# VectorE's last dt step and convolution taps a third of a round later, and VectorE side work in every third of a round

## The chip, the cores and the metric

The kernel runs on one core of a Trainium2 chip (trn2). The metric is device time in microseconds (us): the median of several executions of the same program. A core has five engines that each run their own list of instructions in order: TensorE (PE in the profile), VectorE (DVE), ScalarE (ACT), GpSimd (POOL) and SyncE (SP), which here only issues DMAs. They meet through semaphores.

## The reference

Two layers follow each other on x of shape (8, 384, 32, 32), all in fp32. The first is a group norm, a Mamba block and an MLP, added to x; the second a group norm and a mixture of four experts, of which the two best are used, added again. The change lies in the Mamba block, whose core is:

```python
xz = t @ in_proj_w.T
xm, z = jnp.split(xz, 2, axis=-1)
xc = sum((xp[:, k:k + L, :] * conv_w[:, k] for k in range(K))) + conv_b   # K = 3, causal; xp is xm padded
xc = jax.nn.silu(xc)
dt, Bm, Cm = jnp.split(xc @ x_proj_w.T, [dt_rank, dt_rank + d_state], axis=-1)
dt = jax.nn.softplus(dt @ dt_proj_w.T + dt_proj_b)
dA = jnp.exp(jnp.einsum('bld,dn->bldn', dt, A))
dBu = jnp.einsum('bld,bln->bldn', dt * xc, Bm)
# per token: hst = dA_t * hst + dBu_t ;  y_t = sum over the 16 states of hst * C_t
y = (ys + xc * D) * jax.nn.silu(z)
t = gelu((y @ out_proj_w.T) @ mlp_w1.T + mlp_b1) @ mlp_w2.T + mlp_b2
```

## The kernel before

**Tiling.** The 8 x 1024 tokens are cut into 16 chunks of 512 (`i`; even chunks are the first half of an image, odd ones the second, which start from a carried state). The 768 inner channels are 6 blocks of 128 (`d`), the 16 states 4 groups of 4 (`s`). One round (`r`) is one (chunk, block, state group): 24 rounds (`k`) make a chunk, and the loop has 384 rounds. After it a tail finishes the MLP and the experts' first layer, and `experts` computes the experts' second layer from DRAM.

**One round** scans 4 x 128 rows of 512 tokens. GpSimd multiplies `du = dxr * b` for the next round (`drive`, L742). ScalarE makes four decays exp(dt * A) (`decay`, L734): two into the PSUM tile `da_A`, two one after the other into the single PSUM tile `da_B`, so that the second has to wait for the scan that reads the first. VectorE does four scans (`scan`, L750; the four are numbered j = 0 to 3, of which 2 and 3 use `da_B`) and multiplies half of the result by c (`read_out`, L754); GpSimd does the other half. TensorE sums the states into `y` (`sum_states`, L776) at the head of the next round.

**Side work.** All else (in_proj, convolution, dt, gates, norms, out_proj, MLP, the experts' first layer) is written as generators. Each step `yield`s an engine, a cost and a wait: the wait is the least number of *thirds* of a round after the step before. A round calls `side` three times, at fixed places among the scans:

```python
scan(r, 2); drive(r + 1); decay(r, 3); batch()
side("PE", "DVE", *act, act=ACT_FIRST)          # first third
scan(r, 0); scan(r, 3)
side("PE", *act)                                # middle third
decay(r + 1, 2); scan(r, 1); read_out(V, ...); read_out(G, ...); decay(r + 1, 0); decay(r + 1, 1)
side("PE", "DVE", "ACT", act=ACT_LAST)          # last third
```

`side` gives the named engines credit (2.7 us of TensorE, 0.6 us of VectorE for each third) and issues the steps that are due, the most urgent first. A round in which `batch` has put a Silu or Gelu batch on ScalarE (two table loads and three activations) issues no other ScalarE step in its first two thirds. The order on each engine is therefore fixed when the program is built. A step that opens a PSUM bank ("bank") also needs one of the four banks of `ps_g` to be free at its place in the order; the step that calls `free()` gives it back.

**The two steps that the change touches.** `delta` (L391 and on) makes dt: a matmul into a bank (L396), ScalarE's Relu, Exp and Ln (L400 to L402), then VectorE's `scalar_tensor_tensor` (L404), which gives the bank back. Behind that, GpSimd multiplies dt by xc (`dtx`, L407), and both are written to DRAM and read back repeated. `conv` makes the convolution: three matmuls into a bank (L295), ScalarE's first tap (L307, L308, for even chunks' convolutions also the edge, L311 and L312), then VectorE's two taps (L314, L315), after which the bank is free. Other VectorE side steps are the norm (L267, L283), the additions to x1 (L522 to L528), and the first group norm's statistics (L243).

Of the kernel before, what the change touches and what calls it, by code (L numbers as in the profile page):

```python
# [112 lines left out]
def layer0(ctx, tc, io, ident, cmean, eps, dram, x1_dram, gn1, logits, r_dram, group_norm):  # L113
# [8 lines left out]
    V, S, G, PE = nc.vector, nc.scalar, nc.gpsimd, nc.tensor  # L122
# [68 lines left out]
    def exp_ln_tables():  # L191
        S.preload_act_table_set(EXP_LN_SET)
# [4 lines left out]
    def bank(name):  # L197
        held[0] += 1
        return ps_g.tile([P, T], F32, name=name, tag="g")

    def free():
        held[0] -= 1
# [87 lines left out]
    def in_proj(i, block):  # L290
        assert i in normal
        w = w_in.take("in_proj", block)
        g = bank("g_in")
        for j in range(J):
            PE.matmul(g, lhsT=w[:, j, :], rhs=xt[i][:, j, :], start=(j == 0), stop=(j == J - 1))  # L295
        return g

    def conv(i, d, at_once=False):
        half = i % NH
        while i not in normal or i > 1 and i - 2 not in out_done or not w_in.turn("in_proj", d):  # L300
            yield "-", 0, 1
        yield "bank", 3, 0
        g = in_proj(i, d)
        yield "ACT", 1.1 if half else 1.5, 1
        w = lambda k: conv_w[:, d, k:k + 1]
        acc = pxc.tile([P, T], F32, name="xc")
        S.copy(acc[:, 0:2], (edge if half else edge0)[:, d, :])  # L307
        S.activation(acc[:, 2:T], g[:, 0:T - 2], AF.Identity, bias=conv_b[:, d:d + 1], scale=w(0))  # L308
        if half + 1 < NH:
            e = edge[:, d, :]  # L310
            S.activation(e, g[:, T - 2:T], AF.Identity, bias=conv_b[:, d:d + 1], scale=w(0))  # L311
            S.activation(e[:, 0:1], g[:, T - 1:T], AF.Identity, bias=e[:, 0:1], scale=w(1))  # L312
        yield "DVE", 1.5, 1
        V.scalar_tensor_tensor(acc[:, 1:T], g[:, 0:T - 1], w(1), acc[:, 1:T], ALU.mult, ALU.add)  # L314
        V.scalar_tensor_tensor(acc, g, w(2), acc, ALU.mult, ALU.add)  # L315
        free()
        if at_once:
            yield "ACT", 0.6, 1
            S.activation(acc, acc, AF.Silu)
            xc[i, d] = acc  # L320
        else:
            accs[i, d] = acc
# [51 lines left out]
    def load_b(i, s):  # L374
        bt[i, s] = load_rows("b", i, s)
# [4 lines left out]
    def written(name, i, d, what):  # L380
        there = dram.tile([P, T], F32, name=f"{name}_dram{i}_{d}")
        nc.sync.dma_start(there, what)
        return there

    def repeat(into, there, j):

        rows = there[j * (P // Q):(j + 1) * (P // Q), :]
        nc.sync.dma_start(into, rows.unsqueeze(1).to_broadcast([P // Q, Q, T]))

    def delta(i, d):  # L390
        while i not in dbc or making_dt:  # L391
            yield "-", 0, 1
        making_dt.append((i, d))
        yield "bank", 1, 1
        g = bank("g_dt")
        PE.matmul(g, lhsT=w_dt[:, d * P:(d + 1) * P], rhs=dbc[i][0:DTR, :], start=True, stop=True)  # L396
        projected.add((i, d))
        yield "ACT", 2.0, 1
        dt = p1.tile([P, T], F32, name="dt")
        S.activation(dt, g, AF.Relu, bias=b16[:, d:d + 1], scale=-1.0)  # L400
        S.activation(dt, dt, AF.Exp, bias=top, scale=-1.0)
        S.activation(dt, dt, AF.Ln, bias=1.0)  # L402
        yield "DVE", 0.75, 1
        V.scalar_tensor_tensor(dt, g, b_dt[:, d:d + 1], dt, ALU.add, ALU.max)  # L404
        free()
        dtx = p1.tile([P, T], F32, name="dtx")
        G.tensor_tensor(dtx, dt, xc[i, d], ALU.mult)  # L407
        yield "-", 0, 1
        there = written("dtr", i, d, dt)
        yield "-", 0, 1  # L410
        there_x = written("dxr", i, d, dtx)
        making_dt.clear()
        last = i * per + d * NG - 1
        yield "-", 0, 1
        while issued["B"] < last - NG:
            yield "-", 0, 1
        dtr[i, d] = {}
        pair = dtr[i, d]["B"] = p2.tile([P, 2, T], F32, name="dtr_b")
        for k in range(2):
            repeat(pair[:, k, :], there, 2 + k)  # L420
        yield "-", 0, 1
        while issued["drive"] < last - NG:
            yield "-", 0, 1
        dxr[i, d] = p2.tile([P, Q, T], F32, name="dxr")
        for j in range(Q):
            repeat(dxr[i, d][:, j, :], there_x, j)
        yield "-", 0, 1
        while issued["A"] < last:
            yield "-", 0, 1
        yield "-", 0, 1  # L430
        pair = dtr[i, d]["A"] = p1.tile([P, 2, T], F32, name="dtr_a")
        for k in range(2):
            repeat(pair[:, k, :], there, k)
# [367 lines left out]
    def begin(*new, rank=2):  # L801
        tasks.extend(Task(t, rank) for t in new)
# [66 lines left out]
    with tc.manual_schedule():  # L869
        w_in = Stream(pw_in, [("in_proj", k) for k in in_order()])  # L870
        begin(statistics(0))
        drain()
        begin(norm(0))
        drain()
        S.preload_act_table_set(SILU_SET)
        begin(*(conv(0, d, at_once=True) for d in range(ND)), x_proj(0))
        drain(lambda: len(xc) == ND)
        exp_ln_tables()
        drain()
        load_b(0, 0)  # L880
        load_c(0, 0)
        begin(delta(0, 0))
        drain()
        for s in range(1, NG):
            load_b(0, s)
            load_c(0, s)
        begin(delta(0, 1), rank=0)
        begin(*(gate(0, d) for d in range(3)))
        begin(silus(zs, gates, [(0, d) for d in range(3)]))
        begin(norm(1))  # L890
        w_out = Stream(pw_out, [("out_proj", k) for i in range(NCH) for k in range(2 * J)])
        w_1 = Stream(pw_1, [("mlp_w1", u) for i in range(NCH) for u in range(NF)])
        w_2 = Stream(pw_2, [("mlp_w2", 4 * j + 2 * half + k) for i in range(NCH) for half in range(2)
                            for j in range(J) for k in range(2)])
        seed(0, 0)
        w_e = Stream(pw_e, [("e_w1", u) for i in range(NCH) for u in range(E * J)])
        drive(0)
        for j in (2, 0, 1):
            decay(0, j)
        begin(out_lane(), rank=1.5)  # L900
        begin(hidden_lane(), rank=3)
        begin(second_lane(), rank=2.5)
        begin(expert_lane(), rank=4)

        batched = [False]

        def side(*engines, act=None):
            slot[0] += 1
            credit["PE"] = min(credit["PE"] + PE_SLOT, 4)
            credit["DVE"] = min(credit["DVE"] + DVE_SLOT, 2)  # L910
            if act is not None:
                credit["ACT"] = act + min(credit["ACT"], 0)
            issue({e: ENOUGH[e] for e in engines})

        def batch():

            ready = [t for t in tasks if t.engine == "batch" and t.ready <= slot[0]]
            batched[0] = bool(ready) and not batched[0]
            if batched[0]:
                min(ready, key=Task.urgency).resume()  # L920

        for r in range(rounds):
            i, d, s = at(r)
            k = r % per
            more = r + 1 < rounds
            plan(i, k)
            if r > 0:
                sum_states(r - 1)
            scan(r, 2)
            if more:  # L930
                drive(r + 1)
            decay(r, 3)
            batch()
            act = () if batched[0] else ("ACT",)
            side("PE", "DVE", *act, act=ACT_FIRST)
            scan(r, 0)
            scan(r, 3)
            last_token(G.tensor_copy, r, BB, du[r][:, BB, :])
            side("PE", *act)
            if more:  # L940
                decay(r + 1, 2)
            scan(r, 1)
            read_out(V, r, A, da[r, "A"])
            last_token(V.tensor_copy, r, A, da[r, "A"])
            read_out(G, r, BB, du[r][:, BB, :])
            if more:
                decay(r + 1, 0)
                decay(r + 1, 1)
            if s == 0 and r > 0:
                finish(*at(r - 1)[:2])  # L950
                seed(i, d)
            side("PE", "DVE", "ACT", act=ACT_LAST)
        sum_states(rounds - 1)
        finish(NCH - 1, ND - 1)
        begin(last_x1(), route(), rank=0)
        drain()
# [116 lines left out]
```

## Time and profile before

| what | us |
|---|---|
| three executions: median (lowest to highest) | 4099.31 (4096.35 to 4102.39) |
| profiled execution | 4110.87 |
| its span, first to last instruction | 4109.0 |
| first scan of the loop / first scan of the last round, from the span's start | 76.0 / 3400.0 |
| loop in between, for each of 383 rounds | 8.68 |
| tail (MLP and experts' first layer) | 3400 to 3607 |
| experts' second layer | 3607 to 4109 |

Busy times of the whole span: PE 3709.2, DVE 3032.3, POOL 2782.5, ACT 2422.7 us. A profile's row gives an engine, an instruction, its count, busy time and mean duration, and after the bar the time that its engine sat idle just before it with what ended that idle time. Idle time of an engine costs nothing by itself: what counts is whether the work that waits lies on the path that sets the round's length.

### The profile page before, as it was taken

To read this page: it belongs to the slowest core of one execution; us is meant where nothing else is said; L and a number is where in the kernel's file an instruction comes from. 1 tells how busy PE (TensorE), PEld (TensorE's weight loads), DVE (VectorE), ACT (ScalarE), POOL (GpSimd) and SP (SyncE) were. 2 spreads that over 40 slices of the span, in tenths; PEclk is the share of its full clock that TensorE was granted. 3 is DMA by queue.
4 is the path that set the end of the run, shared out by engine and by line. 5 is a ranking of instruction groups with operands and counts; after the bars stand their busy time and mean duration, and the time that the engine had idled before them with its cause. 6 is when DMAs were issued, how large, how long until landed. Compare 5 with 4: busy or idle time off the path is not lost. (4 is left out here: it accounts for less than half of the span.)

```text
span 4109.0 us, 35186 instructions
## 1 busy us (share of the span) xinstructions
PE 3709.2 (90%) x10294; PEld 1385.4 (34%) x10294; DVE 3032.3 (74%) x3081; ACT 2422.7 (59%) x3762; POOL 2782.5 (68%) x1070
## 2 busy tenths in 40 slices
PE   6678888999999999998999989898999899889999
PEld 2123223333333333333333333333333334334444
DVE  4888888878887878888878787878787781165552
ACT  4657676767686768676766677677767663200000
POOL 3898988788877888888878888888878881000000
PEclk8779898999999999999999999999999999899999
DMA  4444444464545454555455444555554543465552
GB/s 127 134 137 134 152 142 158 143 201 164 172 150 180 164 167 151 192 166 175 154 187 172 159 163 159 181 167 166 165 167 155 163 161 96 169 222 189 185 188 98
DMA packets 372499, 665.31 MB, mean 162 GB/s; under 512 B 40252, under 2 KB 151228, under 8 KB 370132
## 3 DMA queue, kind: packets, MB, share of 16 engines
q1 hardware_dynamic: 342352, 610.02, 45.8%
q10 hardware_dynamic: 29956, 53.05, 3.4%
q8 instruction: 83, 1.36, 0.1%
q14 instruction: 108, 0.88, 0.1%
HBM read 535.90 MB, written 127.01 MB: 161 GB/s over the span
## 5 line engine op out<-in xcount | busy, mean ns | idle before, releaser
L742 POOL TENSOR_TENSOR du<-dxr,b 128x2048 f32<-128x2048 f32 x384 | 1740.9, 4534 | 25.1 <-PE y L776 15.1
L754 POOL TENSOR_TENSOR du<-du,c 128x1024 f32<-128x1024 f32 x384 | 905.8, 2359 | 229.2 <-DVE du L750 199.7
L734 ACT ACTIVATE da_A<-dtr_a,w_a_log 128x512 f32<-128x512 f32 x768 | 527.6, 687 | 280.3 <-DVE du L754 122.1
L734 ACT ACTIVATE da_B<-dtr_b,w_a_log 128x512 f32<-128x512 f32 x768 | 527.3, 687 | 260.4 <-DVE du L750 207.2
L478 PE MATMUL hid<-tt,mlp_w 128*128 128x512 f32 x1152 | 541.5, 613 | 63.8 <-ACT h L482 46.7
L776 PE MATMUL y<-du,sel 128*32 128x512 f32 x3072 | 466.3, 642 | 134.1 <-DVE du L754 92.2
L750 DVE TENSOR_TENSOR_SCAN du<-da_B,carry,du 128x512 f32<-128x512 f32 x384 | 488.4, 1272 | 123.2 <-ACT da_B L734 114.8
L619 PE MATMUL e_hid<-xn,e_w 128*128 128x512 f32 x1080 | 519.2, 627 | 55.4 <-ACT r L623 37.9
L295 PE MATMUL g_in<-xt,in_proj 128*128 128x512 f32 x1152 | 554.7, 619 | 13.8 <-ACT xt L287 7.0
L517 PE MATMUL acc<-h,mlp_w 128*128 128x512 f32 x1152 | 543.4, 614 | 24.5 <-ACT h L493 15.9
L750 DVE TENSOR_TENSOR_SCAN du<-da_B,du 128x512 f32<-128x512 f32 x384 | 464.7, 1210 | 130.5 <-ACT da_B L734 114.0
L1026 PE MATMUL acc<-r,w_e_w 128*128 128x512 f32 x1152 | 496.6, 594 | 13.1 <-DVE r L1023 13.1
L750 DVE TENSOR_TENSOR_SCAN da_A<-da_A,carry,du 128x512 f32<-128x512 f32 x384 | 489.3, 1274 | 9.6 <-ACT da_A L734 9.0
L750 DVE TENSOR_TENSOR_SCAN da_A<-da_A,du 128x512 f32<-128x512 f32 x384 | 465.5, 1212 | 27.0 <-ACT da_A L734 25.0
L754 DVE TENSOR_TENSOR du<-da_A,c 128x1024 f32<-128x1024 f32 x384 | 470.3, 1225 | 13.2
L478 PEld LDWEIGHTS hid<-tt,mlp_w 128*128 128x128 f32 x1152 | 215.8, 193 | 366.5 <-issue 239.1
L517 PEld LDWEIGHTS acc<-h,mlp_w 128*128 128x128 f32 x1152 | 216.6, 195 | 343.9 <-issue 247.7
L295 PEld LDWEIGHTS g_in<-xt,in_proj 128*128 128x128 f32 x1152 | 210.0, 194 | 353.5 <-issue 255.1
L619 PEld LDWEIGHTS e_hid<-xn,e_w 128*128 128x128 f32 x1080 | 207.4, 199 | 356.2 <-issue 250.3
L1026 PEld LDWEIGHTS acc<-r,w_e_w 128*128 128x128 f32 x1152 | 219.6, 191 | 290.1 <-issue 287.3
L456 PE MATMUL g_out<-xc,out_proj 128*128 128x512 f32 x576 | 284.0, 641 | 32.9 <-DVE xc L783 32.9
L407 POOL TENSOR_TENSOR dtx<-dt,xc 128x512 f32<-128x512 f32 x96 | 122.1, 1272 | 217.5 <-DVE dt L404 217.5
(129 smaller groups left out, 3030.2 us busy)
## 6 DMA issues: line engine op xcount, KB each, us to landing
dxr<-dxr_dram SPq DMA_DIRECT2D x384, 256.0 KB, 4.7
mlp_w<-in_mlp_w SPq DMA_DIRECT2D x384, 192.0 KB, 2.9
dtr_b<-dtr_dram SPq DMA_DIRECT2D x192, 256.0 KB, 4.2
dtr_a<-dtr_dram SPq DMA_DIRECT2D x192, 256.0 KB, 3.2
r_dram<-r ACTq DMA_DIRECT2D x192, 256.0 KB, 3.5
r<-r_dram SPq DMA_DIRECT2D x64, 768.0 KB, 4.8
in_proj<-in_in_proj SPq DMA_DIRECT2D x192, 192.0 KB, 4.0
e_w<-in_e_w SPq DMA_DIRECT2D x192, 192.0 KB, 3.2
```

What stands on the lines that cost most here:

```text
L295: PE.matmul(g, lhsT=w[:, j, :], rhs=xt[i][:, j, :], start=(j == 0), stop=(j == J - 1))
L407: G.tensor_tensor(dtx, dt, xc[i, d], ALU.mult)
L456: PE.matmul(g, lhsT=w[:, d, :], rhs=xc[i, 3 * k + d], start=(k + d == 0), stop=(k == 1 and d == 2))
L478: PE.matmul(g, lhsT=w[:, j, :], rhs=tt[i][:, j, :], start=(j == 0), stop=(j == J - 1))
L517: PE.matmul(g, lhsT=w[:, n, :], rhs=hs[mine[n]], start=(k + n == 0), stop=(k == 1 and n == 2))
L619: PE.matmul(h, lhsT=w[:, j, :], rhs=xn[:, j, :], start=(j == 0), stop=(j == J - 1))
L734: S.activation(out, dtr[i, d][pair][:, j % 2, :], AF.Exp, scale=neg_a[:, d, j, s:s + 1])
L742: G.tensor_tensor(du[r], dxr[i, d], wide(bt[i, s].unsqueeze(1), [P, Q, T]), ALU.mult)
L750: V.tensor_tensor_scan(a if j < 2 else b, a, b, start, ALU.mult, ALU.add)
L754: engine.tensor_tensor(du[r][:, js, :], h, wide(ct[i, s].unsqueeze(1), [P, 2, T]), ALU.mult)
L776: PE.matmul(y[j * m:(j + 1) * m, :], lhsT=sel, rhs=h[:, j, :], start=False, stop=(s == NG - 1), tile_position=(0, j * m), skip_group_check ...
L1026: PE.matmul(acc[j], lhsT=e2[:, e, d, j, :], rhs=r[:, d, :], start=(e + d == 0), stop=(e + d == E + J - 2))
```

## The change

`conv`'s and `delta`'s VectorE steps wait two thirds of a round behind ScalarE's step where they waited one, and the middle third of a round may issue VectorE steps too.

```diff
@@ conv
             S.activation(e[:, 0:1], g[:, T - 1:T], AF.Identity, bias=e[:, 0:1], scale=w(1))
-        yield "DVE", 1.5, 1
+        yield "DVE", 1.5, 2
         V.scalar_tensor_tensor(acc[:, 1:T], g[:, 0:T - 1], w(1), acc[:, 1:T], ALU.mult, ALU.add)
         V.scalar_tensor_tensor(acc, g, w(2), acc, ALU.mult, ALU.add)
         free()
@@ delta
         S.activation(dt, dt, AF.Ln, bias=1.0)
-        yield "DVE", 0.75, 1
+        yield "DVE", 0.75, 2
         V.scalar_tensor_tensor(dt, g, b_dt[:, d:d + 1], dt, ALU.add, ALU.max)
         free()
@@ the loop over rounds
             last_token(G.tensor_copy, r, BB, du[r][:, BB, :])
-            side("PE", *act)
+            side("PE", "DVE", *act)
             if more:
                 decay(r + 1, 2)
```

## The prediction

> **What bounds the kernel now.** I read the busy times by stretch, then who waited for whom inside the loop, then single rounds. The stretches are first scan to last (76 to 3400 us), tail, and experts' second layer (us; then busy us and instruction count of PE, PEld, DVE, ACT, POOL; granted clock, DMA share, GB/s):
>
> ```profile
> 76.00:3400.00 3324.00, 2994.14 (x8645) 1073.60 (x8646) 2720.27 (x2698) 2332.43 (x3612) 2771.78 (x1053) 0.95 0.50 163
> 3400.00:3607.00 207.00, 172.54 (x410) 74.16 (x409) 27.46 (x54) 61.96 (x93) 2.76 (x3) 0.90 0.43 145
> 3607.00:4109.00 502.00, 496.38 (x1152) 219.33 (x1152) 266.45 (x303) 0.00 (x0) 0.00 (x0) 0.99 0.51 171
> ```
>
> In the loop TensorE is busy 90%, GpSimd 83%, VectorE 82%, ScalarE 70%: none is full, all are near it, and a round of 8.68 us on average is longer than the 7.08 us (4.53 + 2.36 + 0.19) that GpSimd's own row sums ask. What lies between is waiting. VectorE's and GpSimd's waits in the loop:
>
> ```profile
> DVE du L750 <- ACT da_B L734: 228.4, 234, 3.9
> DVE dt L404 <- ACT dt L402: 153.3, 80, 4.1
> DVE xc L314 <- ACT edge L312: 57.9, 29, 3.2
> DVE xc L314 <- ACT xc L308: 49.9, 36, 2.6
> ...
> POOL du L754 <- DVE du L750: 195.1, 106, 5.0
> POOL dtx L407 <- DVE dt L404: 160.0, 78, 4.5
> POOL carry L759 <- DVE du L750: 150.7, 89, 4.1
> ...
> PE y L776 <- DVE du L754: 92.2, 45, 6.5
> ```
>
> VectorE stands 153.3 + 57.9 + 49.9 = 261 us before the steps that the change moves, and GpSimd 160 us before dtx. These sums invite a forecast of -260 us. Two timelines say what a wait is worth. First round 9 of chunk 8, VectorE and ScalarE (start, duration, idle before in brackets):
>
> ```profile
> 1800.77 1.21 DVE L750 TENSOR_TENSOR_SCAN du<-da_B,du 128x512 f32<-128x512 f32 x1
> 1803.41 0.75 DVE L314 SCALAR_TENSOR_TENSOR xc<-g_in,w_conv_w,xc 128x511 f32<-128x511 f32 x1 [1.43 <-ACT xc L308]
> ...
> 1804.86 1.22 DVE L750 TENSOR_TENSOR_SCAN da_A<-da_A,du 128x512 f32<-128x512 f32 x1
> ...
> 1808.35 1.23 DVE L754 TENSOR_TENSOR du<-da_A,c 128x1024 f32<-128x1024 f32 x1
> ...
> 1802.60 0.78 ACT L308 ACTIVATE xc<-g_in,w_conv_b,w_conv_w 128x510 f32<-128x510 f32 x1
> 1803.27 0.69 ACT L734 ACTIVATE da_B<-dtr_b,w_a_log 128x512 f32<-128x512 f32 x1
> ```
>
> VectorE waits 1.43 us for the convolution's first tap, and ScalarE makes the decay of scan 3 only behind that tap. Then the end of round 17, a dt step:
>
> ```profile
> 1880.06 0.75 DVE L404 SCALAR_TENSOR_TENSOR dt<-g_dt,w_dt_b,dt 128x512 f32<-128x512 f32 x1 [3.00 <-ACT dt L402]
> 1881.99 1.22 DVE L750 TENSOR_TENSOR_SCAN du<-da_B,du 128x512 f32<-128x512 f32 x1 [1.19 <-ACT da_B L734]
> 1883.26 1.23 DVE L750 TENSOR_TENSOR_SCAN da_A<-da_A,du 128x512 f32<-128x512 f32 x1
> ```
>
> The scan behind dt waits as well, for a decay that stands behind Relu, Exp and Ln.
>
> **What the Trainium skill says.** "TensorE: Matmul & The Clock Gate", on the array and its queues (Architectural detail), has ScalarE's and VectorE's queues as strict FIFO. The trace agrees: 3.00 us at dt held a scan and everything else behind it. "Perfetto Trace Analysis", Optimizing Tensor Performance, Matmuls, wants matmul groups to rotate through PSUM banks so that evacuation of one overlaps the next; here four banks are shared, and the change holds two kinds of bank longer. "ScalarE: Activation LUTs", What ACT_TABLE_LOAD costs, gives 1283 ns for a table load; the trace's row has 1283 ns too.
>
> **The change part by part.** It adds and removes no instruction: the built orders hold the same ones, and the tail keeps all of its matmuls (36 hidden, 36 second, 48 expert, 18 out_proj). Only waits can change, within the 3324 us. The orders show:
>
> - dt, 95 times in the loop: 80 move from the last third to the first of the next round, thus behind scan 2; 15 from a first third to the middle one, behind scans 0 and 3. GpSimd's dtx moves behind the 4.53 us drive.
> - convolution taps, 90: 58 first and 32 last thirds become 20 first, 50 middle, 20 last.
> - the x1 additions, norm and statistics spread over the three thirds; the DMA writes of dt come one third later on SP, and for 7 chunks the next chunk's first dt about a round later, at round 19 where its data is read from round 23: two rounds or more of cover, for transfers of 4.7 us.
>
> *Convolution.* In round 9 above, in the new order: scan 0 follows scan 2 (to 1803.1), the decay for scan 3 is there at 1803.96, scan 3 ends at 1805.25, the taps (0.75 + 0.75) at 1806.75, scan 1 at 1807.9. The read-out starts there and not at 1808.35: -0.45 us. So of 1.43 us of wait a third is gained; the rest comes back as a wait for `da_B`. Walking rounds 6 to 12 this way by hand, with the rows' durations and both orders, from the end of round 5: the even chunk takes 64.4 us in the old order (64.5 in the trace) and 62.3 in the new, the odd one 1.0 less. 8 even and 7 odd chunks: -16 - 7 = -23 us. The walk takes TensorE and GpSimd as in time.
>
> *dt.* In round 17's case scan 2 still starts at 1881.99, dt follows at 1883.2, scan 0 at 1883.95 where it was at 1883.26: +0.7. Done for the 81 dt steps that stand before scan 2, leaving out the very first, single values run from -0.7 to +2.9 (gain positive) and the sum is a loss of 9 us: the wait for Ln becomes one for the decay right behind Ln. Half of these lie beside a ScalarE or TensorE path; I take +5, with 0 and +57 (81 x 0.7) as ends.
>
> *GpSimd.* Its 160 us at dtx go, but the read-out that follows needs scan 3, and 195 + 151 us of waits for it show who is late. Only in rounds 0 to 4 of odd chunks, at 7.0 us a round, is GpSimd the path: 0.7 us there, 7 times: -5. Ends 0 and -40 (a quarter of 160).
>
> *The norm.* In odd chunks the dt of round 22 and the norm's 1.81 us stand together behind one wait (round 22 takes 12.1 us). Apart, the norm fills that wait: about -1.4, 7 times: -10.
>
> *The later dt of even chunks.* Round 17 (11.8 us on average) loses it, but rounds 18 and 19 get it and four groups of expert matmuls in one round: I put the three, 30.5 us before in chunk 8, at 29.5 at least. Seven times -1: -7, ends -21 and +14.
>
> *Banks.* dt's and the convolution's banks come back a third (2.9 us) later. In the built orders all four banks are held at the end of 326 thirds where it was 207, and a TensorE group opens a bank freed in the same third, with no other free, 177 times where it was 86 (behind dt 40 for 7, behind taps 30 for 6). These 91 add a wait of TensorE on VectorE. No row shows its price: nothing if TensorE is behind anyway, as between rounds 12 and 21; one scan and dt, about 2 us, if it is in step. With half out of sight and 0.4 for the others: 91 x 0.2 = +18. Ends 0 and +91 (1.0 each). What hides them is TensorE's lag; where that is gone, y is late and the read-out's buffer with it.
>
> Sum: -23 + 5 - 5 - 10 - 7 + 18 = -22 us. The profiled execution takes 4110.9 (1.9 outside its span), which would become 4089; it stood 11.6 above the median of the runs, so the forecast for the median is 4077 us. Without the guessed terms it is -23 - 10, with them at their worst +129 (57 + 14 + 91 - 33).
>
> **The rivals.**
>
> *TensorE starves at the banks.* The place is the first and middle thirds, where a group now opens a bank that VectorE has just given back. TensorE has 330 us of idle time in the loop, 10%, so waits land on it soon; in favour also that single rounds get more uneven (in chunk 8 round 18 keeps 2 us of matmuls and 19 gets 12). Against: in sums over two rounds the loads of both orders agree within 0.2%. The other terms give -40, so it decides from 40/91 = 0.44 us for each added case; at 0.9 us the time is 4099 - 40 + 82 = 4141.
>
> *The waits go for good.* If scans had their decays ready whenever VectorE passes dt and taps, the 261 us would go; about 110 would return as waits for `da_B` (half of 228): 4099 - 150 = 3950. The two timelines speak against it.
>
> *Nothing measurable.* TensorE, whose groups fill rounds 12 to 21, sets the time, and the gains are waited out there: 4099. About 0.2% (8 us) is what a measurement of this kernel tells from no change.
>
> *The change doesn't do what it says:* excluded by the built orders.
>
> **How the numbers follow.** The forecast, 4077 with 4045 to 4091 around it, gets 0.44; waits gone for good (below 4040) 0.07; nothing 0.12; the banks, or dt on the path at its upper end, 0.37, from 4108 up. So faster 0.51, same 0.12, slower 0.37. For 8 in 10 the range is 4010 to 4150: a tenth is left below, and above it only the bank term at its full price with dt's.
>
> **What would show it.** Right: the waits at L404 and L314 nearly gone, dtx without wait, `da_B` waits of VectorE up by some 100 us, rounds 6 to 12 of even chunks 2 us shorter. Wrong in the sum: TensorE's matmul waits behind `dt L404`, 20 us now, and behind taps grown by over 40 us; or `da_B` waits grown by more than 261 us, the moved waits and more.

## The result, and the profile after

The changed kernel takes 4063.81 us (median of 6, 4055.27 to 4069.07) beside 4097.83 us for the kernel before on the same chip (6, 4093.61 to 4102.65): a ratio of 0.9913, with a 95% interval of 0.9899 to 0.9927, or 34 us less. The forecast was 4077.

The busy times by stretch for the kernel after, in the columns of the prediction's first fence:

```profile
76.00:3359.00 3283.00, 2975.97 (x8646) 1079.95 (x8647) 2715.10 (x2699) 2328.63 (x3613) 2775.44 (x1054) 0.95 0.50 165
3359.00:3565.00 206.00, 169.75 (x409) 72.63 (x408) 27.39 (x53) 61.65 (x93) 2.56 (x2) 0.93 0.43 147
3565.00:4067.00 502.00, 496.70 (x1152) 219.46 (x1150) 266.43 (x303) 0.00 (x0) 0.00 (x0) 0.99 0.50 171
```

All of the gain lies in the loop, 3324 us before and 3283 now; the tail (207 and 206 us) and the experts' second layer (502) stay. The instructions are the same and the busy times move little, most of all TensorE's, by 18 us of 2994. So it is mainly waits that went. Here are waits of VectorE, GpSimd and TensorE in the loop, after:

```profile
DVE du L750 <- ACT da_B L734: 416.6, 283, 5.8
...
POOL du L742 <- PE y L776: 55.8, 39, 4.2
POOL dtx L407 <- ACT da_B L734: 32.9, 29, 2.8
...
PE e_hid L619 <- DVE dt L404: 4.2, 5, 0.9
PE g_in L295 <- DVE dt L404: 3.9, 6, 0.7
```

The waits in front of dt (L404) and the taps (L314), 261 us before, are gone from the list, but the scans' wait for `da_B` rose by 188 us (228.4 to 416.6). GpSimd's 160 us in front of dtx became 54 us (33 of them put down to a decay), and its wait in front of the drive, for TensorE's `y`, grew from 15 to 56 us. Some 370 us of waits left their places, and the loop of this profile is 41 us shorter.

Round 9 of chunk 8, the prediction's example, now reads like this on VectorE and ScalarE:

```profile
1781.91 1.21 DVE L750 TENSOR_TENSOR_SCAN du<-da_B,du 128x512 f32<-128x512 f32 x1
...
1785.35 1.22 DVE L750 TENSOR_TENSOR_SCAN du<-da_B,du 128x512 f32<-128x512 f32 x1 [1.11 <-ACT da_B L734]
1786.49 0.72 DVE L314 SCALAR_TENSOR_TENSOR xc<-g_in,w_conv_w,xc 128x511 f32<-128x511 f32 x1
...
1789.17 1.23 DVE L754 TENSOR_TENSOR du<-da_A,c 128x1024 f32<-128x1024 f32 x1
...
1783.95 0.78 ACT L308 ACTIVATE xc<-g_in,w_conv_b,w_conv_w 128x510 f32<-128x510 f32 x1
1784.63 0.69 ACT L734 ACTIVATE da_B<-dtr_b,w_a_log 128x512 f32<-128x512 f32 x1
```

The taps find their data, and scan 3 waits 1.11 us for the decay that stands behind ScalarE's first tap. From the first scan to the read-out it is 7.26 us; it was 7.58 before.

Where the rounds changed is told by the start of each round's first scan. These are means over chunks 2 to 14, in us, of the four kernels that the explanation needs most, each from one profile. (The profiled execution of the kernel before took 4110.9 us, 13 above the median, so its column is somewhat long.)

| rounds | before, even / odd | after, even / odd | e2, even / odd | e12, even / odd |
|---|---|---|---|---|
| 0 to 4 | 41.4 / 36.0 | 37.9 / 40.1 | 40.3 / 36.0 | 39.9 / 36.0 |
| 5 | 11.0 / 10.1 | 10.4 / 10.8 | 10.2 / 10.1 | 10.3 / 10.1 |
| 6 to 12 | 62.0 / 65.5 | 59.9 / 64.9 | 59.0 / 63.4 | 59.0 / 63.5 |
| 13 to 16 | 32.0 / 33.1 | 32.7 / 34.2 | 31.8 / 33.5 | 31.8 / 33.5 |
| 17 to 20 | 38.0 / 37.4 | 35.1 / 38.3 | 37.8 / 37.0 | 35.0 / 37.0 |
| 21 to 23 | 26.5 / 28.6 | 26.4 / 26.4 | 26.0 / 28.6 | 26.2 / 29.0 |
| chunk | 210.9 / 210.6 | 202.3 / 214.7 | 205.1 / 208.6 | 202.1 / 209.1 |

Even chunks gained 8.6 us each and odd ones lost 4.1. The change touches both alike, so something that differs between them must carry much of the result. The built orders show what: in even chunks of the kernel after, norm's mean comes in round 23 where it was 22, the next chunk's first dt in round 19 where it was 17, and in odd chunks norm's last additions in round 5 where they were in round 1. Nothing in the diff asks for that; it follows from the planner.

### The profile page after: what moved, and what is told of

It is laid out like the page before. It is cut to its first block, busy times and chain, and to the rows that moved or that the text cites. A ratio compares the mean times of both kernels' runs of the same rounds, so it can differ in the third digit from the quotient of the medians.

```text
span 4067.3 us, 35077 instructions
## 1 busy us (share of the span) xinstructions
PE 3688.2 (91%) x10294; PEld 1390.4 (34%) x10294; DVE 3026.9 (74%) x3081; ACT 2418.6 (59%) x3762; POOL 2785.6 (68%) x1070
## 5 line engine op out<-in xcount | busy, mean ns | idle before, releaser
L295 PE MATMUL g_in<-xt,in_proj 128*128 128x512 f32 x1152 | 561.3, 626 | 28.9 <-ACT xt L287 23.4
L517 PE MATMUL acc<-h,mlp_w 128*128 128x512 f32 x1152 | 535.8, 612 | 26.2 <-ACT h L482 15.9
L478 PE MATMUL hid<-tt,mlp_w 128*128 128x512 f32 x1152 | 529.8, 601 | 21.6 <-ACT h L482 10.2
L1023 DVE TENSOR_TENSOR r<-r,spread 128x1536 f32<-128x1536 f32 x64 | 112.4, 1756 | 198.3 <-DMA r<-r_dram 182.5
```

Of the source, the lines that this page charges most:

```text
L478: PE.matmul(g, lhsT=w[:, j, :], rhs=tt[i][:, j, :], start=(j == 0), stop=(j == J - 1))
L517: PE.matmul(g, lhsT=w[:, n, :], rhs=hs[mine[n]], start=(k + n == 0), stop=(k == 1 and n == 2))
L1023: V.tensor_tensor(r4, r4, wide(spread[i][:, :, e, :].unsqueeze(1), [P, J, TT, P]), ALU.mult)
```

## The experiments

All times are medians beside the kernel before on the same chip, whose medians beside these runs were 4097 to 4098. The first eight runs take the change apart, the last four the order that came with it.

**e1: the middle third alone.** Both waits as in the kernel before.

```diff
-            side("PE", *act)
+            side("PE", "DVE", *act)
```

> Only the middle third may issue VectorE steps; both waits stay at one third. In the built order dt stays where it was (79 of 95 in the last third) and of 90 convolutions 7 reach the middle third; mostly the additions to x1 move. Theory 1 (the gain is the taps behind scans 0 and 3): no more than 8 us either way, 4090 to 4106. Theory 2 (the gain is the spreading of all side work): 4065 to 4080. Theory 3 (the gain is the next chunk's first dt at round 19 of even chunks): 4098, as it stays at round 17.

Measured: 4086.00, ratio 0.997 (0.9959 to 0.9981; 15 runs). Opening the middle third is worth 12 us.

**e2: the middle third and the convolution's wait.**

```diff
@@ conv
-        yield "DVE", 1.5, 1
+        yield "DVE", 1.5, 2
@@ the loop over rounds
-            side("PE", *act)
+            side("PE", "DVE", *act)
```

> Middle third and the convolution's wait of two; dt as before. 56 of 90 convolutions stand in the middle third, dt stays in the last third, the first dt of the next chunk stays at round 17. Theory 1: -23 us and a little, about 4070 to 4078, with the waits at L314 gone and rounds 6 to 12 shorter by 1 to 2 us. Theory 2: as e1. Theory 3: 4098.

Measured: 4050.09, ratio 0.9884 (0.9868 to 0.99). The convolution's wait brings another 36 us, and without dt's part the kernel is faster than the whole change. Round 9 of chunk 8 on VectorE, first in e1:

```profile
1784.59 1.21 DVE L750 TENSOR_TENSOR_SCAN du<-da_B,du 128x512 f32<-128x512 f32 x1
1787.90 0.75 DVE L314 SCALAR_TENSOR_TENSOR xc<-g_in,w_conv_w,xc 128x511 f32<-128x511 f32 x1 [2.10 <-ACT xc L308]
...
1792.83 1.22 DVE L754 TENSOR_TENSOR du<-da_A,c 128x1024 f32<-128x1024 f32 x1
```

and in e2:

```profile
1770.86 1.21 DVE L750 TENSOR_TENSOR_SCAN du<-da_B,du 128x512 f32<-128x512 f32 x1
...
1773.16 1.22 DVE L750 TENSOR_TENSOR_SCAN du<-da_B,du 128x512 f32<-128x512 f32 x1
1774.30 0.72 DVE L314 SCALAR_TENSOR_TENSOR xc<-g_in,w_conv_w,xc 128x511 f32<-128x511 f32 x1
...
1776.98 1.22 DVE L754 TENSOR_TENSOR du<-da_A,c 128x1024 f32<-128x1024 f32 x1
```

From first scan to read-out it was 8.24 us and is 6.12: here all of the 2.10 us is gained. Over rounds 6 to 12, six convolutions, 2.7 us remain in even chunks and 3.2 in odd ones (61.7 and 66.6 us in e1). Scan 0 ran while ScalarE made its tap and the decay behind it, and scan 3 at 1773.16 found that decay ready. In the kernel after, the same order gained 0.3 us on the kernel before, where e2 gains 1.5; there ScalarE reached its tap later: 2.04 us behind the start of scan 2, where in e2 it was 0.90 us. What a removed wait is worth depends on how early the other engine is.

**e3: the middle third and dt's wait.**

```diff
@@ delta
-        yield "DVE", 0.75, 1
+        yield "DVE", 0.75, 2
@@ the loop over rounds
-            side("PE", *act)
+            side("PE", "DVE", *act)
```

> Middle third and dt's wait of two; the convolution as before. dt stands in the first third of the next round, the next chunk's first dt at round 18 in all chunks. Theory 1: dt behind scan 2 costs 5 us and the norm apart from dt gains up to 10: 4088 to 4105, the wait at L404 gone and come back as a wait for da_B. Theory 2: as e1. Theory 3: 4098 or a little below, as the first dt moves by a third only.

Measured: 4128.17, ratio 1.0076 (1.0063 to 1.0089). This is slower than before, and 42 us slower than e1, from which its edit differs in dt's wait alone. At the turn from round 5 to 6 of chunk 8, VectorE in e1:

```profile
1756.39 0.75 DVE L404 SCALAR_TENSOR_TENSOR dt<-g_dt,w_dt_b,dt 128x512 f32<-128x512 f32 x1 [2.36 <-ACT dt L402]
...
1759.24 1.21 DVE L750 TENSOR_TENSOR_SCAN du<-da_B,du 128x512 f32<-128x512 f32 x1
1760.37 1.21 DVE L750 TENSOR_TENSOR_SCAN da_A<-da_A,du 128x512 f32<-128x512 f32 x1
...
1766.26 1.22 DVE L750 TENSOR_TENSOR_SCAN du<-da_B,du 128x512 f32<-128x512 f32 x1 [0.54 <-ACT da_B L734]
```

and in e3:

```profile
1785.95 1.21 DVE L750 TENSOR_TENSOR_SCAN du<-da_B,du 128x512 f32<-128x512 f32 x1
1787.08 0.72 DVE L404 SCALAR_TENSOR_TENSOR dt<-g_dt,w_dt_b,dt 128x512 f32<-128x512 f32 x1
1787.72 1.22 DVE L750 TENSOR_TENSOR_SCAN da_A<-da_A,du 128x512 f32<-128x512 f32 x1
...
1793.01 1.21 DVE L750 TENSOR_TENSOR_SCAN du<-da_B,du 128x512 f32<-128x512 f32 x1
```

In e1 dt's step stands in a time in which VectorE waits for ScalarE. In e3 it stands between scans 2 and 0, which start 1.77 us apart where it was 1.13. But the round is no longer for that: scan 2 of round 7 waits 0.54 us for its decay in e1 and not in e3, and from scan 2 to scan 2 it is 7.02 and 7.06 us. The means say the same, for rounds 5 to 12 take as long in e3 as in e1 (72.8 us in even chunks, 76.7 in odd ones). So this is not where the 42 us come from. They lie mostly in two other places: rounds 0 to 4 of even chunks take 42.6 us (39.5 in e1), and rounds 13 to 16 of odd chunks 36.6 (31.6 in e1), nearly all of that in round 13. That round of chunk 9 in e1, TensorE and VectorE:

```profile
2031.02 2.74 PE L517 MATMUL acc<-h,mlp_w 128*128 128x512 f32 x6
...
2033.79 0.75 DVE L522 SCALAR_TENSOR_TENSOR x<-acc,w_mlp_b,x 128x512 f32<-128x512 f32 x1 [0.34 <-PE acc L517]
```

and in e3:

```profile
2062.12 1.23 PE L358 MATMUL g_x<-xc,w_x_proj 128*56 128x512 f32 x2 [2.46 <-ACT z L331]
2063.27 4.33 PE L517 MATMUL acc<-h,mlp_w 128*128 128x512 f32 x6
...
2067.64 0.75 DVE L522 SCALAR_TENSOR_TENSOR x<-acc,w_mlp_b,x 128x512 f32<-128x512 f32 x1 [3.60 <-PE acc L517]
```

The round takes 7.93 us in e1 and 12.82 in e3, and in e3 no dt step of VectorE stands in it. TensorE waits 2.46 us for ScalarE's copy of z, which gives back a bank where x_proj (L358) opens one, and then makes six matmuls of the MLP in 4.33 us where they took 2.74; VectorE waits 3.60 us for them in front of the addition to x1, with scan 1 behind it. Here the loss is TensorE's lateness, in an order that dt's longer wait has changed; for rounds 0 to 4 I can't name the cause.

**e4: both waits, middle third closed.**

```diff
@@ conv
-        yield "DVE", 1.5, 1
+        yield "DVE", 1.5, 2
@@ delta
-        yield "DVE", 0.75, 1
+        yield "DVE", 0.75, 2
```

> Both waits of two, no VectorE step in the middle third. Convolutions go to the last third (71 of 90), so their banks are held longest: four held in 358 thirds against 326 with the whole change. The first dt of the next chunk stands at round 19 of even chunks. Theory 1: the taps are not behind scan 0 and 3 of their own round but at its end, before the next scan 2: gain lost, banks dearer: 4095 to 4130. Theory 2: no spreading, 4098 or above. Theory 3: the gain stays, 4065 to 4075.

Measured: 4061.16, ratio 0.9915 (0.99 to 0.993), as good as the whole change. Rounds 6 to 12, where the convolutions are, take 61.3 us in even chunks and 61.9 in odd ones (62.0 and 65.5 before), so the taps gain without a middle third to stand in. The whole time isn't clean evidence, since this order has norm and the first dt late too.

**e5: the whole change, with norm and the first dt early again.** The statistics that the planner ranked last get a higher rank; norm's mean then comes in round 21 and the first dt in round 18.

```diff
-            begin(statistics(i // NH + 1), rank=3)
+            begin(statistics(i // NH + 1), rank=2)
```

> The whole change, with the first group norm's statistics begun at rank 2 and not 3, so that they are issued sooner. In the built order the norm and the next chunk's first dt stand early again (norm at rounds 19 to 25 as before, first dt at round 18), while dt stays behind scan 2 and the convolution in the middle third. Theory L (with dt's wait the norm comes late, and that costs the odd chunks their +4 us in rounds 0 to 4, while the late first dt gains 2.7 in rounds 17 to 20 of even chunks): odd chunks near 210, 4045 to 4060. Theory D (dt's place behind scan 2 itself costs): 4064 or more, up to 4092 (e2 plus the 42 us between e1 and e3).

Measured: 4100.06, ratio 1.0004 (0.9996 to 1.0012). Without the order that came with it the change gains nothing that can be measured: that order is worth 36 us, all of the gain. e5 and e2 put the taps into nearly the same thirds (26, 51 and 13 of them against 26, 56 and 8), so the 50 us between them price dt's move a second time, with the statistics' rank and an earlier norm in the sum. Part of it is the step's own length. Round 6 of chunk 8 in e2:

```profile
1744.83 1.22 DVE L750 TENSOR_TENSOR_SCAN du<-da_B,du 128x512 f32<-128x512 f32 x1 [1.29 <-ACT da_B L734]
...
1747.40 1.22 DVE L750 TENSOR_TENSOR_SCAN da_A<-da_A,du 128x512 f32<-128x512 f32 x1
```

and in e5:

```profile
1769.14 1.22 DVE L750 TENSOR_TENSOR_SCAN du<-da_B,du 128x512 f32<-128x512 f32 x1 [4.51 <-ACT da_B L734]
1770.29 0.73 DVE L404 SCALAR_TENSOR_TENSOR dt<-g_dt,w_dt_b,dt 128x512 f32<-128x512 f32 x1
...
1772.37 1.22 DVE L750 TENSOR_TENSOR_SCAN da_A<-da_A,du 128x512 f32<-128x512 f32 x1
```

Between the two scans stand the taps in both and dt in e5 alone: 2.57 and 3.23 us. Here it stays, and the round takes 7.86 and 8.52 us. In e2 dt had stood in the wait in front of scan 2. Rounds 6 to 12 of even chunks take 1.9 us more in e5 than in e2; the rest of the 50 lies elsewhere.

**e6: e2, with GpSimd's dtx a third later, behind the drive.**

```diff
         free()
+        yield "-", 0, 1
         dtx = p1.tile([P, T], F32, name="dtx")
         G.tensor_tensor(dtx, dt, xc[i, d], ALU.mult)
-        yield "-", 0, 1
```

> e2 with GpSimd's dtx issued a third later than VectorE's dt, so behind the drive. Its wait at dtx (153 us in e2's loop) should go. Prediction's theory (GpSimd is not on the path): within 8 us of e2's 4050, its waits for scan 3 grown by most of the 153. Rival (the wait before the drive counts): 4050 less a quarter or more of 153, 4010 or below.

Measured: 4052.76, ratio 0.9879 (0.9863 to 0.9895). GpSimd's waits in the loop, e2:

```profile
POOL du L754 <- DVE du L750: 172.6, 93, 4.6
POOL dtx L407 <- DVE dt L404: 153.1, 82, 3.9
POOL carry L759 <- DVE du L750: 108.9, 90, 3.0
```

and e6:

```profile
POOL du L754 <- DVE du L750: 228.2, 122, 4.6
POOL carry L759 <- DVE du L750: 182.2, 124, 4.4
...
POOL dtx L408 <- DVE dt L404: 7.3, 6, 1.2
```

146 us of wait went from dtx, and 129 came back in front of the carry and the read-out, which wait for the scans. The time doesn't move: GpSimd's wait at dtx cost nothing that can be measured.

**e7: the convolution's wait alone.**

```diff
@@ conv
-        yield "DVE", 1.5, 1
+        yield "DVE", 1.5, 2
```

> Only the convolution's wait of two, without the middle third. 71 of 90 convolutions stand in the last third, before scan 2 of the next round; first dt at round 19 and norm late as in e4. If dt's wait costs by itself, this is below e4's 4061, by 10 to 40 us; if it doesn't, 4055 to 4068. If the gain of the convolution needs the place behind scans 0 and 3 (theory 1 as written), 4098.

Measured: 4070.24, ratio 0.9926 (0.9912 to 0.994), 27 us less than before. Here too the order has both late, so I read the stretch: rounds 6 to 12 take 61.0 and 63.2 us, 1.0 and 2.3 less than before. With e4 this speaks against a theory that needs the taps behind scans 0 and 3: what seems to pay is that VectorE does something else while ScalarE makes its first tap.

**e8: dt's wait alone.**

```diff
@@ delta
-        yield "DVE", 0.75, 1
+        yield "DVE", 0.75, 2
```

> Only dt's wait of two, without the middle third. dt in the first third of the next round 86 times, norm late, first dt at round 18. Prediction's term: +5 us, 4098 to 4108. If dt's place costs what e3 has over e1: 4130 to 4145; with a late norm on top up to 4170.

Measured: 4100.65, ratio 1.0005 (0.9996 to 1.0014). dt's move seems free here, and costs 42 us in e3. The orders differ: e8's norm comes late, as in the kernel after, and e3's doesn't. In e8, even chunks' rounds 0 to 4 fall to 38.3 us (41.4 before) and odd ones' rise to 38.6 (36.0); odd chunks' rounds 13 to 16, where e3 loses most, take 34.0 (33.1).

**e9 to e11: which part of the late order gains.** Three theories: A, the late first dt; B, the late norm; C, the whole order of the chunk, with x_proj and the Silu and Gelu batches. e9 puts the first dt of e5 a round later in even chunks:

```diff
-            if k == 17:
+            if k == 17 + (i % 2 == 0):
                 begin(delta(n, 0), rank=0)
```

> The kernel of e5 (4100) with one thing put back: in even chunks the next chunk's first dt (g_dt L396, dt L400 to L404, dtx) comes a round later, as in the changed kernel; norm stays early. Theory A, that the late first dt is what made the changed kernel's even chunks short: their rounds 17 to 20 lose 3 us in each of 7 or 8 chunks (38.3 to about 35), so about 4078. Theory B, that the late norm is the cause: no change, 4100. Theory C, that it is the whole order of the chunk that moves with norm (x_proj, the z gates' Silu batch against the MLP's Gelu batch): 4100 too.

Measured: 4083.79, ratio 0.9965 (0.9953 to 0.9978), 16 us less than e5. Rounds 17 to 20 of even chunks take 36.0 us, in e5 38.3. e10 begins norm a round later instead:

```diff
-        if k == 21 and n + 1 < NCH:
+        if k == (22 if i % 2 == 0 else 21) and n + 1 < NCH:
             begin(norm(n + 1))
```

> The kernel of e5 with norm begun one round later in even chunks: norm's mean and its additions come late (rounds 23 and, in the odd chunk behind, up to 3), the Silu and Gelu batches and x_proj keep their places of e5, and the first dt stays early. Theory A (late first dt): 4100, no gain. Theory B (late norm): about 4066 to 4080, seen in even chunks' rounds 0 to 4 (42.2 to about 38). Theory C (the order of batches and x_proj): 4100.

Measured: 4082.41, ratio 0.9963 (0.995 to 0.9975), 18 us less than e5, but not where it was expected: even chunks' rounds 0 to 4 keep 42.5 us, and odd chunks fall from 210.7 to 206.9. e11 is e10 with 23 in place of 22, after which the planner makes nearly the order of the kernel after.

> The kernel of e5 with norm begun two rounds later in even chunks: the planner then puts norm, x_proj, the Silu and Gelu batches and the first dt where the changed kernel has them, while the statistics keep e5's order of rank. All of theories A, B and C: about 4064, the changed kernel's time, with even chunks near 202 us. If it stays at 4100 the gain lies in the rank of the statistics itself, and none of the three holds.

Measured: 4070.97, ratio 0.9935 (0.9923 to 0.9948), 29 us less than e5, and 7 us above the kernel after, with which its interval overlaps. A late first dt and a late norm are each worth about half of the 36 us. Theory A has its gain where it foretold it; B doesn't. C alone, which foretold 4100 for e9 and e10, is out. Why a late norm helps odd chunks in e10 and even ones in e11 is open.

**e12: e2 with the late first dt.**

```diff
@@ conv
-        yield "DVE", 1.5, 1
+        yield "DVE", 1.5, 2
@@ the loop over rounds
-            side("PE", *act)
+            side("PE", "DVE", *act)
@@ the begins of a round
-            if k == 17:
+            if k == 17 + (i % 2 == 0):
                 begin(delta(n, 0), rank=0)
```

> e2 (convolution's wait and the middle third, 4050) with the first dt a round later in even chunks, norm and all else in place. Theory A: rounds 17 to 20 of even chunks 37.8 to about 35, 20 us less, about 4030. Theories B and C: 4050, no change.

Measured: 4027.20, ratio 0.9824 (0.9811 to 0.9837), 23 us less than e2 and the best of all kernels here, 37 us below the kernel after. In the table above e12 differs from e2 almost only in rounds 17 to 20 of even chunks, 37.8 to 35.0 us. Round 17 of chunk 8 in e2, on VectorE, ScalarE and TensorE:

```profile
1843.52 0.15 DVE L759 COPY carry<-da_A 128x2 f32<-128x2 f32 x1
1846.67 0.75 DVE L404 SCALAR_TENSOR_TENSOR dt<-g_dt,w_dt_b,dt 128x512 f32<-128x512 f32 x1 [3.00 <-ACT dt L402]
1848.61 1.22 DVE L750 TENSOR_TENSOR_SCAN du<-da_B,du 128x512 f32<-128x512 f32 x1 [1.19 <-ACT da_B L734]
...
1844.54 0.69 ACT L400 ACTIVATE dt<-g_dt,b 128x512 f32<-128x512 f32 x1 [3.97 <-POOL du L754]
...
1839.59 2.82 PE L478 MATMUL hid<-tt,mlp_w 128*128 128x512 f32 x6
1842.34 1.07 PE L776 MATMUL y<-du,sel 128*32 128x512 f32 x8
1843.33 1.12 PE L396 MATMUL g_dt<-dbc,w_dt_proj 24*128 24x512 f32 x2
```

TensorE has hidden-layer matmuls of the MLP to finish, then the state sums, and makes dt's matmul last, to 1844.45. ScalarE stands 3.97 us in front of Relu with the next decay behind it, and VectorE waits 3.00 and 1.19 us. The profile names GpSimd as what released Relu; by the times it was the matmul, which ended 0.09 us before it. The same place in e12:

```profile
1837.16 0.15 DVE L759 COPY carry<-da_A 128x2 f32<-128x2 f32 x1
1838.17 1.22 DVE L750 TENSOR_TENSOR_SCAN du<-da_B,du 128x512 f32<-128x512 f32 x1 [0.85 <-ACT da_B L734]
...
1847.89 0.67 ACT L400 ACTIVATE dt<-g_dt,b 128x512 f32<-128x512 f32 x1
...
1843.32 1.12 PE L396 MATMUL g_dt<-dbc,w_dt_proj 24*128 24x512 f32 x2
```

Round 18's first scan starts 1.01 us after the copy where it took 5.09. dt's matmul comes a round later and is done, at 1844.44, long before ScalarE reaches Relu at 1847.89, so ScalarE doesn't stand. Part comes back in round 19, where dt still makes VectorE wait for 2.06 us; rounds 17 to 20 of this chunk take 36.8 us against 38.9.

**A rival that these runs don't separate: TensorE's clock.** The profile shows the clock that TensorE was granted, as a share of full speed. Its mean over a kernel's runs is 0.952 both before and after, 0.954 in e1 and 0.955 in e2, so it doesn't explain the whole change or the convolution's part. But it is 0.946 in e3 (e1: 0.954), 0.947 in e5 (e2: 0.955), and 0.949, 0.949 and 0.953 in e9 to e11, and so moves with what I ascribe to dt's move and to a late norm. It moves with the rounds too: in rounds 0 to 4, as a mean over chunks 2 to 14, even chunks have 0.90 before and 0.99 after, odd ones 0.97 and 0.90, and it is there that even chunks gained 3.5 us and odd ones lost 4.1. In those rounds of chunk 8 it is 0.88 in e3 and 0.96 in e1, and twelve out_proj matmuls take 8.40 us in e3 that take 5.42 in e1; in e3's round 13 above it is 0.87, in e1's 1.00. TensorE's busy time in the whole loop is only 11 us larger in e3 than in e1, where the loops of these profiles differ by 45. Whether the lower clock makes the waits or the waits come first and the clock follows, no run tells.

## Why the prediction came near, and where its steps failed

**The sum.** -34 us came and -22 was forecast. From kernel to kernel the runs give: middle third -12 (e1), convolution -36 (e2), dt's move with norm and first dt early +50 (e5), the late order -36 (the kernel after). That the sum is right is partly luck: errors of both signs met. The parts are not independent: the convolution's wait brought 27 us alone (e7), 36 beside the middle third (e2), and 39 on top of dt's wait (e8 to e4), and only the middle one of these leaves norm and the first dt in place.

**Convolution, -23.** The walk put rounds 6 to 12 at -2.1 us in even chunks and -1.0 in odd ones; the profile after has -2.1 and -0.6, times 8 and 7 that is 21 us. This step was right, and as a net value: the convolution's own part is larger (e1 to e2: -2.7 and -3.2 in these rounds), and dt takes back 1.9 us of it in even chunks there (59.0 in e2, 60.9 in e5).

**dt, +5.** This term was mis-sized: e3 shows +42, and e5 against e2 +50. The step that failed is "Half of these lie beside a ScalarE or TensorE path; I take +5". What the walk priced, dt's 0.7 us in front of scan 0, does occur; in e3's rounds 5 to 12 it costs nothing by the end of the round, and in e5 it is 0.66 us in round 6 of even chunks. The largest part of e3's loss is TensorE's lateness in rounds 13 to 16 of odd chunks (5.0 us in each), which no term priced: this one counts VectorE's own step, and the bank term only banks that VectorE gives back. The next, 3.1 us in rounds 0 to 4 of each even chunk, stays open. That the term's upper end, +57 from 81 x 0.7, came near is luck. On strict order in ScalarE's and VectorE's queues, the Trainium skill's "TensorE: Matmul & The Clock Gate", Architectural detail, is borne out again: in e5, with dt away, 4.51 us of wait stand at the next instruction in line, scan 2.

**GpSimd, -5.** e6 puts it at nothing within its interval. The places where GpSimd was said to be the path, odd chunks' rounds 0 to 4, take 36.0 us in both e2 and e6 (7.2 us a round and not 7.0). Its wait at dtx went for the most part, as foretold: 54 us are left of 160.

**The norm, -10.** Odd chunks' rounds 21 to 23 fell from 28.6 to 26.4 us, 7 times -2.2 or -15, by dt's move: e3 has 26.1 there and e1 28.5. Its size was a little low. But that norm itself moves in even chunks wasn't priced, and its lateness is worth some 18 us (e10), by a way that stays open.

**The later first dt, -7.** e9 gives -16 and e12 -23, near the end value of -21. The step put chunk 8's rounds 17 to 19 at 29.5 us at least. They took 23.4 in the kernel after; 2.9 us of that came back in round 20 (10.0 to 12.9). What was mis-sized is TensorE's lag: four groups of matmuls in one round were counted as a load on round 18 and not as time for dt's matmul to be ready.

**Banks, +18.** In the kernel after nothing of it shows. TensorE's matmul waits behind dt, 20 us before, are the 8 us shown above, and its idle time in the loop, by the stretches, fell from 330 to 307 us. That TensorE was late at the 91 added openings anyway, the prediction's lower end, would fit this; no run isolates the term. In e3 and e5 a wait for a bank does show: the 2.46 us above, in six odd chunks, and 1.75 us at the same place in e5, each time for a bank that ScalarE gives back and not VectorE. So the page's wish for rotating banks (the Trainium skill, "Perfetto Trace Analysis", Optimizing Tensor Performance, Matmuls) has its case in those two orders, and shows no price in this one.

**The signs named ahead.** The waits at dt and taps went, and rounds 6 to 12 fell by 2 us. The `da_B` waits grew by 188 us where some 100 were expected, under the 261 that would have meant a loss. That sign was too coarse: up to 3330 us e5 has 455.6 us of them and e12 266.2, but e2, with 280.2, and e7, with 282.5, lie 20 us apart.

**The rivals.** The waits going for good (3950) and a starved TensorE (4141) didn't come. The slower side was given to banks or dt's upper end; e3, dt's move without the convolution's, is 30 us slower than before, with TensorE waiting for a bank in the round that loses most.

## What to carry to other kernels

In engines that work in order, ask of each wait what stands behind it: moving the waiting step helps when the time is then filled (e2, 2.1 us in one round, some 3 over seven). It can cost the step's own length when the step was itself filling a wait that stays (e5 beside e2, 0.66 us), or nothing when the next wait takes it up (e3, round 6). And follow a scan or two further before you multiply: the largest part of e3's 42 us lay in a round where TensorE came late, and not where dt's step had gone. Wait sums don't price a change: 261 us of VectorE's waits went for 34 us, and 146 us of GpSimd's for nothing. Where a planner makes the order, compare the built orders for what moves unasked, and then move that alone; here one dt a round later, by one line, was worth 23 us, as much as two thirds of the whole change.

## What the runs showed of the hardware that was not expected

A DMA issued from ScalarE's queue holds the decay behind it. In round 9 of chunk 8 of the kernel after, on ScalarE, with VectorE's scan 2 of round 10 below:

```profile
1790.44 0.67 ACT L623 ACTIVATE r<-e_hid,w_e_b 128x512 f32<-128x512 f32 x1
1791.14 0.35 ACTq L624 DMA_DIRECT2D r_dram<-r  x1
1791.54 0.69 ACT L734 ACTIVATE da_B<-dtr_b,w_a_log 128x512 f32<-128x512 f32 x1 [0.43 <-ACT r L623]
...
1792.33 1.22 DVE L750 TENSOR_TENSOR_SCAN du<-da_B,du 128x512 f32<-128x512 f32 x1 [1.87 <-ACT da_B L734]
```

The issue starts when the activation before it has ended, takes 0.35 us, and the decay starts behind it, 0.43 us after ScalarE was last busy, while VectorE waits 1.87 us for that decay. The program has 192 such writes. No run moved them to another queue, so what they cost stays open.
